# Audio tower layer: the feed-forward part in quads of sequences, or in rounds over a ring of pairs

## Chip, cores, metric

One core of a Trainium2 chip. The metric is the device time of one launch in microseconds (us). Four compute engines run side by side, each through its own queue in order: PE (matmul), DVE (vector), ACT (activation functions), POOL; SP issues the DMA transfers, also in order.

## What is computed

32 audio sequences of 313 frames of 512 samples go through a DCT, one retention-like attention block and one feed-forward block, each with a layernorm before it and a residual around it. The feed-forward block is what takes the time:

```python
h = tokenize(x)                                   # frames (32, 313, 512) times a 512x512 DCT
h = h + attn(layernorm(h))                        # 8 heads of 64, softmax times a decay matrix
y = layernorm(h)
theta = y[..., None, :] / (1 + abs(W)) + B_param  # (32, 313, 256, 512)
idx = mod(round(theta * 4096 / (2 * pi)), 4096)
cos_sum = sum(cos_table[idx] * attn_cos, axis=-1) # (32, 313, 256)
sin_sum = sum(sin_table[idx] * attn_sin, axis=-1)
h = h + silu(cos_sum @ proj_cos_w.T + sin_sum @ proj_sin_w.T)
```

So each of 256 hidden units needs a sine and a cosine of every feature of every frame: 32 x 313 x 512 x 256 x 2 = 2.6 billion function values.

## The kernel before

**Layout.** Features lie on the 128 partitions, in four chunks (NC4); frames lie along the free dimension. The 32 sequences are eight quads of four, so a chunk of a quad is a tile row of T = 4 x 313 = 1252 frames.

**Feed-forward, `ffn` (L538).** For each of 256 units n: four DVE operations (L556), one per chunk, turn `xT` (float32) into int16 indices with the unit's scale and bias per feature, `f_scale` and `f_bias`; L563 masks them to 12 bits for the sine; L568 and L574 add a quarter turn and mask again for the cosine, into a second buffer. ACT takes the sine of each whole buffer of 4 x 1252 = 5008 elements (L581). PE multiplies by `hot`, weights that are zero outside one column of 32 (L591), so that 32 units gather in one PSUM bank, each sequence in its own 32 rows. After 32 units DVE copies two banks out (L603) and SP stores them to `sums_d` in DRAM (L609). There are four index buffers, three of sine results, two of `hot`, four banks.

**Attention (`attention`, L293) and output (`output`, L493).** One sequence at a time: frames into `a5`, DCT (helper `rows`, L275), copy into `h` (L210), layernorm (L234, its inverse square root on POOL, L226 to L229), transpose, `xnT`, values `v`, gate, then two halves of four heads (`columns`, L289; scores L352; maxima L360; exponentials L378; transposes L399; decay L411; product with v L417), group norm (L440 to L456), the product with the gate, projection, residual (L475), a second layernorm, and the transposed result through `a5` to `xT_d` in DRAM. `load_xT` (L532) later reads a whole quad of it. The four copies out of PSUM into `h`, `xnT`, `v` and `a5` run on ACT (`ENG_H` and its like). `output` reads the sums back and finishes a sequence.

**Order.** Every step is entered into a `Plan` (L46) with a key, an engine, an estimated duration and the buffers that it reads and writes. `emit` (L63) runs through these once and fixes each engine's order: of the steps whose inputs would be ready, the one with the lowest key. The key of unit n of quad q is 512 q + 2 n, so a key step is one sine of 5008 elements. In `tile_audio_tower` the attention of quad 0 comes first, with two sets of buffers, A and B, two sequences at a time (L689). Then B's memory becomes that of the feed-forward part (`swap`, L692). While quad q is in the feed-forward part, attention of the four sequences of quad q+1 is spread over the keys between 30 and 482 of its 512 (L704); the last quad has no attention beside it.

Of the kernel before, what the change touches and what calls it, by code (L numbers as in the profile page):

```python
# [28 lines left out]
QUAD = 4  # L29
# [10 lines left out]
ENG_H = "ACT"  # L40
ENG_XNT = "ACT"
ENG_V = "ACT"
ENG_A5 = "ACT"
# [83 lines left out]
def tile_audio_tower(ctx: ExitStack, tc: tile.TileContext, t: dict, out: bass.AP):  # L127
    nc = tc.nc
    n_quads = t["frames"].shape[0]
    S = t["frames"].shape[4]  # L130
    T = QUAD * S
# [7 lines left out]
    out_v = out.rearrange("(a b) s d -> a b s d", b=QUAD)  # L139
# [9 lines left out]
    xT_d = dram.tile([P, NC4, T], F32, name="xT_d")  # L149
    sums_d = dram.tile([2, P, 2, T], F32, name="sums_d")  # L150
    wv_d = dram.tile([NC4, P, HOP], F32, name="wv_d")
    h_d = dram.tile([n_quads, QUAD, S, HOP], F32, name="h_d")

    class Buffers:


        def __init__(self, name, pool, psum):
# [8 lines left out]
            self.a5 = sb("a5", NC4, S)  # L166
            self.h = sb("h", NT, HOP)
            self.xn = sb("xn", NT, HOP)
            self.xnT = sb("xnT", NC4, S)
            self.v = sb("v", NT, HOP)  # L170
            self.gate = sb("gate", NC4, S)
            self.qk = [sb(f"qk{i}", 2, S) for i in range(2)]
            self.raw = sb("raw", 2, S)
            self.prob = sb("prob", NB, NT, S)
            self.probT = sb("probT", NT, S)
            wide = self.prob.rearrange("p a b s -> p (a b s)")
# [105 lines left out]
    def columns(plan, key, x, bank, src):  # L282

        k = x.load(plan, key, src)

        def go():
            w = x.ring[k].rearrange("p (c n) -> p c n", n=P)
            for c in range(NC4):
                nc.tensor.matmul(x.W[:, bank, :S], w[:, c, :], x.xnT[:, c, :],  # L289
                                 start=(c == 0), stop=(c == NC4 - 1))  # L290
        plan.add(key, "PE", 2200, go, (x.k("xnT"), x.k("ring", k)), x.banks(bank))

    def attention(plan, keys, q, b, x):  # L293
# [4 lines left out]
        def step(n=1.0):  # L298
            done[0] += n
            return keys(done[0] / 139.0)  # L300

        xns, probs = x.every("xn", NT), x.every("prob", NB)
        W3 = x.W[:N, :NT, :]
        plan.add(step(0), "SP", DMA_NS, lambda: nc.sync.dma_start(x.a5, t["frames"][q, b]), (),
                 (x.k("a5"),))
        rows(plan, step(7), x, x.a5, t["dct"], (x.k("a5"),))
        copy(plan, step(), ENG_H, NT * HOP, x.h[:N], W3, x.banks(0, 1, 2), (x.k("h"),))
        layernorm(plan, step(3), x)
        transposed(plan, step(3), x)
        copy(plan, step(), ENG_XNT, NC4 * S, x.xnT, x.W[:, :, :S], x.banks(0, 1, 2, 3), (x.k("xnT"),))  # L310
# [4 lines left out]
        copy(plan, step(), ENG_V, NT * HOP, x.v[:N], W3, x.banks(0, 1, 2), (x.k("v"),))  # L315
        plan.add(step(0), "POOL", 500, lambda: nc.gpsimd.memset(x.v[0:1, : NT - 1, :], 0.0), (),
                 (x.k("v"),))


        key = step(6)  # L320
        for g in range(NC4):
            columns(plan, key, x, g, t["wg"][g])
        plan.add(step(), "ACT", 1270,
                 lambda: nc.scalar.activation(x.gate, x.W[:, :, :S], AF.Silu),
                 x.banks(0, 1, 2, 3), (x.k("gate"),))

        for hb in range(H // NB):
            for g in range(hb * NB // 2, (hb + 1) * NB // 2):
                key = step(4)
                qk = x.qk[g % 2]  # L330
                kq = x.k("qk", g % 2)
# [12 lines left out]
                plan.add(key, "DVE", 1640, turned, x.banks(2, 3), (x.k("raw"), kq))  # L344
            for hd in range(hb * NB, (hb + 1) * NB):
                key = step(2.5)
                a, r0 = hd % NB, (hd % 2) * DH
                qk, kq = x.qk[hd // 2 % 2], x.k("qk", hd // 2 % 2)
# [39 lines left out]
            for hd in range(hb * NB, (hb + 1) * NB):  # L388
# [25 lines left out]
                for i in range(NT):  # L414
# [8 lines left out]
                    plan.add(key, "PE", 1000, go, (x.k("probT"), x.k("v")), x.banks(3))  # L423
# [9 lines left out]
                )  # L433

# [29 lines left out]
        for c in range(NC4):  # L464
# [6 lines left out]
                 lambda: nc.vector.tensor_tensor(x.gate, x.gate, x.aff, ALU.mult), probs,  # L471
                 (x.k("gate"),))
        rows(plan, step(7), x, x.gate, t["wo"], (x.k("gate"),))
# [18 lines left out]

    def output(plan, key, q, b, x):  # L493

        probs, xns = x.every("prob", NB), x.every("xn", NT)

        def load():
            for m in range(2):
# [328 lines left out]
```

## Time and profile before

| | |
|---|---|
| median of 3 runs | 19,201.89 us (19,189.18 to 19,209.79) |
| the profiled execution | 19,200.94 us, its span 19,199.2 us |
| ACT busy | 18,323.5 us (95%) |
| DVE busy | 17,754.5 us (92%) |
| PE busy | 14,967.9 us (78%) |
| DMA queue of SP | 806.95 MB, 14.3% of 16 engines' span |
| granted TensorE clock | 0.913 |

A row of the groups gives line, engine and operation, tiles written and read, shapes, count, then busy time in us and mean ns of one, then how long the engine sat idle just before such operations and what ended that. Successive operations of an engine overlap a little, so a mean is longer than the distance between two starts. The timeline gives start and length in us.

### The profile page before, as it was taken

What the parts mean: (1) busy time and instruction counts of PE and PEld (TensorE: products, weight loads), DVE (VectorE), ACT (ScalarE), POOL (GpSimd) and SP (SyncE); (2) the same over time, 40 slices, a digit from 0 to 9 for tenths busy, and PEclk for the clock granted to TensorE, in tenths of its full rate; (3) what the DMA queues carried; (4) which work ended last, traced back from release to release, by engine and by line L of the source; (5) the groups of instructions that cost most, each with busy time, mean ns of one, the idle gap of its engine ahead of it and who ended that gap; (6) DMA issues with size and microseconds to landing.
All of it is one profiled execution on the core that took longest, in us unless ns stands there. A gap on an engine that the chain in (4) does not pass through costs nothing.

```text
span 19199.2 us, 336270 instructions
## 1 busy us (share of the span) xinstructions
PE 14967.9 (78%) x148864; PEld 6732.7 (35%) x148864; DVE 17754.5 (92%) x17005; ACT 18323.5 (95%) x6051; POOL 581.0 (3%) x1222
## 2 busy tenths in 40 slices
PE   8777777887787877888777887788787777877666
PEld 5433333333333333333333333333333333322222
DVE  3799999999999999999999999999999999999997
ACT  1699999999999999999999999999999999999998
POOL 0000000000000000000000000000000000000000
PEclk8899999999999998999989999899999999987898
DMA  3111111111121111111111111111111111110001
GB/s 92 51 40 39 40 41 59 42 42 41 34 65 40 40 42 38 58 42 43 40 57 37 42 43 41 57 41 39 39 43 61 39 40 41 39 49 17 18 18 37
DMA packets 455954, 828.47 MB, mean 43 GB/s; under 512 B 54208, under 2 KB 103360, under 8 KB 454496
## 3 DMA queue, kind: packets, MB, share of 16 engines
q1 hardware_dynamic: 454496, 806.95, 14.3%
q8 instruction: 1169, 19.15, 0.4%
q14 instruction: 289, 2.37, 0.0%
HBM read 723.64 MB, written 83.10 MB: 42 GB/s over the span
## 4 chain that ended last, share of the span: by engine, by line
ACT 36%; DVE 33%; PE 17%; issue 11%; POOL 3%; DMA 0%; DVEq 0%; ACTq 0%; SPq 0%; POOLq 0%
ACT trig L581 34%; DVE ix L556 13%; PE pa L591 11%; DVE ix L563 5%; DVE ix L568 5%; DVE ix L574 5%; PE a_W L275 2%; PE a_W L289 2%; ACT a_prob L378 1%; DVE a_mx L360 1%; PE a_W L417 1%; PE a_W L352 1%; DVE a_prob L369 1%; POOL a_lu L226 1%; DVE a_st L238 0%
## 5 line engine op out<-in xcount | busy, mean ns | idle before, releaser
L581 ACT ACTIVATE trig<-ix 128x5008 f32<-128x5008 int16 x4096 | 17522.7, 4368 | 201.0 <-DVE ix L563 132.8
L591 PE MATMUL pa<-trig,hot 128*32 128x313 f32 x131072 | 10546.7, 468 | 3449.9 <-ACT trig L581 3433.5
L591 PEld LDWEIGHTS pa<-trig,hot 128*32 128x32 f32 x131072 | 4114.7, 117 | 9466.3 <-ACT trig L581 5200.6
L556 DVE TENSOR_SCALAR ix<-xT,f_scale,f_bias 128x1252 int16<-128x1252 f32 x8192 | 7108.7, 927 | 331.0 <-ACT trig L581 326.9
L568 DVE TENSOR_SCALAR ix<-ix 128x5008 int16<-128x5008 int16 x2048 | 3006.7, 1468 | 206.5 <-ACT trig L581 15.6
L563 DVE TENSOR_SCALAR ix<-ix 128x5008 int16<-128x5008 int16 x2048 | 2999.5, 1465 | 68.3
L574 DVE TENSOR_SCALAR ix<-ix 128x5008 int16<-128x5008 int16 x2048 | 3004.2, 1467 | 61.7
L289 PE MATMUL a_W<-a_xnT,a_ring 128*128 128x313 f32 x4800 | 1402.1, 437 | 92.2 <-DVE a_qk L338 66.6
L289 PEld LDWEIGHTS a_W<-a_xnT,a_ring 128*128 128x128 f32 x4800 | 873.3, 190 | 618.3 <-issue 156.1
L275 PE MATMUL a_W<-a_ring,a_a 128*105 128x512 f32 x1488 | 700.1, 612 | 27.5 <-DMA a_ring<-in_dct 15.4
L417 PEld LDWEIGHTS a_W<-a_v,a_probT 105*105 105x105 f32 x4320 | 482.7, 188 | 316.7 <-issue 187.5
L417 PE MATMUL a_W<-a_v,a_probT 105*105 105x64 f32 x4320 | 546.2, 277 | 41.1 <-DVE a_probT L411 41.0
L352 PE MATMUL a_W<-a_qk 64*105 64x313 f32 x1440 | 481.2, 459 | 100.8 <-DVE a_prob L369 75.9
L399 PE MATMUL a_W<-ident,a_prob 105*105 105x105 f32 x2160 | 350.4, 305 | 234.2 <-ACT a_prob L378 216.4
L275 PE MATMUL a_W<-a_ring,a_gate 128*105 128x512 f32 x720 | 377.0, 643 | 70.5 <-DVE a_gate L471 70.5
L399 PEld LDWEIGHTS a_W<-ident,a_prob 105*105 105x105 f32 x2160 | 282.0, 205 | 393.8 <-ACT a_prob L378 260.9
L275 PEld LDWEIGHTS a_W<-a_ring,a_a 128*105 128x105 f32 x1488 | 241.4, 173 | 419.4 <-issue 400.7
L275 PE MATMUL a_W<-a_ring,a_xnT 128*105 128x512 f32 x720 | 354.0, 616 | 2.8 <-ACT a_xnT L210 2.8
L226 POOL TENSOR_TENSOR a_gu<-a_gr 105x24 f32<-105x24 f32 x90 | 48.5, 539 | 10147.2 <-DVE a_gr L220 10142.5
L352 PEld LDWEIGHTS a_W<-a_qk 64*105 64x105 f32 x1440 | 224.1, 173 | 361.2 <-DVE a_prob L369 146.5
L262 PE MATMUL a_W<-ident,a_xn 105*128 105x105 f32 x1080 | 177.7, 291 | 172.5 <-DVE a_xn L250 90.1
L378 ACT ACTIVATE a_prob<-a_prob 105x313 f32<-105x313 f32 x540 | 242.6, 451 | 67.2 <-DVE a_prob L369 66.5
(136 smaller groups left out, 4029.3 us busy)
## 6 DMA issues: line engine op xcount, KB each, us to landing
hot<-in_hot SPq DMA_DIRECT2D x1024, 256.0 KB
a_dec<-in_decay SPq DMA_DIRECT2D x240, 260.5 KB
a_ring<-in_proj SPq DMA_DIRECT2D x128, 256.0 KB
a_ring<-in_dct SPq DMA_DIRECT2D x120, 256.0 KB
a_ring<-wv_d SPq DMA_DIRECT2D x120, 256.0 KB
a_ring<-in_wg SPq DMA_DIRECT2D x120, 256.0 KB
a_ring<-in_wq SPq DMA_DIRECT2D x120, 256.0 KB
a_ring<-in_wk SPq DMA_DIRECT2D x120, 256.0 KB
```

What stands on the lines that cost most here:

```text
L275: lambda c=c, i=i, k=k, to=to: nc.tensor.matmul(x.W[:N, to, :], lhsT[:, c, ROW0[i] : ROW0[i] + N], x.ring[k], start=(c == 0), stop=(c == N ...
L289: nc.tensor.matmul(x.W[:, bank, :S], w[:, c, :], x.xnT[:, c, :], start=(c == 0), stop=(c == NC4 - 1))
L352: lambda i=i, qk=qk, r0=r0: nc.tensor.matmul(x.W[:N, i, :S], qk[r0 : r0 + DH, 0, ROW0[i] : ROW0[i] + N], qk[r0 : r0 + DH, 1, :], start=Tru ...
L378: nc.scalar.activation(x.prob[:N, a, i, :], x.W[:N, i, :S] if last else x.prob[:N, a, i, :], AF.Exp, bias=m[:N, i : i + 1] if last else 0. ...
L399: nc.tensor.transpose(x.W[:N, jj, ROW0[i] : ROW0[i] + N], x.prob[:N, a, i, ROW0[j] : ROW0[j] + N], ident[:N, :N],)
L417: nc.tensor.matmul(x.y[:N, i, (hd % 2) * DH : (hd % 2 + 1) * DH], x.probT[:N, jj, ROW0[i] : ROW0[i] + N], x.v[:N, jj, hd * DH : (hd + 1) * ...
L556: nc.vector.tensor_scalar(now["ix", x][:, c, :], now["xT", c], f_scale[:, c, n : n + 1], f_bias[:, c, n : n + 1], ALU.mult, ALU.add)
L563: nc.vector.tensor_scalar(now["ix", x], now["ix", x], LUT - 1, LUT // 2, ALU.bitwise_and, ALU.bitwise_xor)
L568: nc.vector.tensor_scalar(new("ix", y, [P, NC4, T], I16, bufs=N_IX), now["ix", x], float(LUT // 4), None, ALU.add)
L574: nc.vector.tensor_scalar(now["ix", x], now["ix", x], LUT - 1, None, ALU.bitwise_and)
L581: nc.scalar.activation(new("trig", w, [P, NC4, T], bufs=N_TRIG), now["ix", x], AF.Sin, bias=-PI32, scale=ANG)
L591: nc.tensor.matmul(now["pa", p][b * 32 : b * 32 + 32, :S], now["hot", z][:, n % 2, c, k, :], now["trig", w][:, c, b * S : (b + 1) * S], st ...
```

## The change

**A ring of pairs.** A sequence pair is now the unit that enters. A ring has four places (`RING` = 8 sequences), each chunk of `xT` being one tile of 8 x 313 frames. The feed-forward part runs in rounds; a round takes 32 units (`UNITS`) for all pairs that stand in the ring, and a pair stays for eight rounds, that is 256 units, beginning with whichever block of 32 comes next. Pair p joins at round `STARTS[p]`: rounds 0 to 3 hold one pair, 4 to 9 two, 10 to 13 three, 14 to 35 four, 36 and 37 three, 38 and 39 two, 40 and 41 one. In rounds 36 to 39 an empty place lies between the pairs.

**Tile shapes in a round.** A buffer still has room for 16 x 313 = 5008 elements. With one pair it holds all eight combinations of four chunks and two units, with two pairs four of them, with four pairs two (one chunk, two units). With three pairs it also holds two, and so 3756 elements. An index operation covers all pairs of a chunk that are neighbours in the ring.

**Attention.** Only the first two sequences are done ahead, then `swap`. Buffers are shared: `u` takes the place of `a5`, `gate` and `qk`; `v` lies in `h`; `raw` in `probT`. Since `v` overwrites `h`, `h` is stored to DRAM after the DCT and read back after the heads; the gate is computed after the heads. The four copies out of PSUM run on DVE (`mover`), save for sequences whose attention begins while one pair is in the ring. `f_scale` and `f_bias` are computed in `prob`, stored to DRAM as `f_d` in eight blocks, and each round loads its block. Keys of attention are spread so that each pair is ready eight keys before its round; outputs stand before the next attention that begins.

```diff
-QUAD = 4
+RING = 8
+UNITS = 32
+SLOT = 16
+STARTS = (0, 4, 8, 10, 12, 14, 16, 18, 20, 22, 24, 26, 28, 30, 32, 34)
...
-            self.a5 = sb("a5", NC4, S)
+            self.u = sb("u", NC4, S)
+            self.qk = [self.u[:, 2 * i : 2 * i + 2, :] for i in range(2)]
             self.h = sb("h", NT, HOP)
+            self.v = self.h
...
+            self.raw = self.probT[:, 0:2, :]
...
-        copy(plan, step(), ENG_H, NT * HOP, x.h[:N], W3, x.banks(0, 1, 2), (x.k("h"),))
+        copy(plan, step(), mover, NT * HOP, x.h[:N], W3, x.banks(0, 1, 2), (x.k("h"),))
+        residual(step(0), False)
...
+        residual(step(0), True)
+        key = step(6)
+        for g in range(NC4):
+            columns(plan, key, x, g, t["wg"][g])
...
+    def ffn_round(plan, k0, blk, ring):
+        pairs = [(at, pair) for at, pair in enumerate(ring) if pair is not None]
+        r = 2 * len(pairs)
+        runs = []
+        for j, (at, _) in enumerate(pairs):
+            if runs and runs[-1][0] + runs[-1][2] == at:
+                runs[-1][2] += 1
+            else:
+                runs.append([at, j, 1])
+        n_p = min(SLOT // r, 2 * NC4) if SLOT % r == 0 else 2
+        E = n_p * r * S
...
+        for n in range(0, UNITS, 2):
...
+            todo = [(c, u) for c in range(NC4) for u in range(2)]
+            for i in range(n_slots):
+                parts = todo[i * n_p : (i + 1) * n_p]
...
+                                    nc.vector.tensor_scalar(
+                                        now["ix", x][:, d0 : d0 + 2 * m * S],
+                                        now["xT", c][:, 2 * at * S : 2 * (at + m) * S],
+                                        f[:, 0, c, n + u : n + u + 1], f[:, 1, c, n + u : n + u + 1],
+                                        ALU.mult, ALU.add)
...
+                        nc.scalar.activation(tl[:, :E], now["ix", x][:, :E], AF.Sin,
+                                             bias=-PI32, scale=ANG)
...
+                    key += n_p * r / SLOT
...
-    for b in range(QUAD):
-        attention(plan, lambda x: -1000.0 + b // 2 + x, 0, b, (A, B)[b % 2])
+    for b in range(2):
+        attention(plan, lambda x: -1000.0 + x, b, (A, B)[b], "ACT")
...
+    times, p, k = [], 1, 0.0
+    while p < len(STARTS):
+        due = [(key_of[STARTS[q]] - 8.0 - k) / (q - p + 1) for q in range(p, len(STARTS))]
+        for _ in range(int(np.argmin(due)) + 1):
+            times += [k, k + min(due) / 2]
+            k += min(due)
+            p += 1
...
+        narrow = sum(q is not None for q in rings[int(np.searchsorted(key_of, k, "right")) - 1]) <= 1
+        events.append((k, 1, lambda k=k, e=e, i=i, narrow=narrow: attention(
+            plan, lambda x: k + (e - k) * x, 2 + i, A, "ACT" if narrow else "DVE")))
```

With these keys the windows of attention are 60 keys for each of the sequences 2 and 3 (keys 0 to 120), 81 to 96 for 4 to 11 (to key 888), 113 or 128 for 12 to 31 (to key 3448). Round 4 begins at key 128, round 8 at 384, round 10 at 512, round 14 at 896, round 34 at 3456; the last round ends at 4096.

## The prediction

> **What bounds the kernel now.** I read the page's first two parts, then the groups by line, then the busy time in stretches, the timeline at the start and in the middle, and the waits inside the loop.
>
> ```profile
> PE 14967.9 (78%) x148864; PEld 6732.7 (35%) x148864; DVE 17754.5 (92%) x17005; ACT 18323.5 (95%) x6051; POOL 581.0 (3%) x1222
> ...
> L581 ACT ACTIVATE trig<-ix 128x5008 f32<-128x5008 int16 x4096 | 17522.7, 4368 | 201.0 <-DVE ix L563 132.8
> L556 DVE TENSOR_SCALAR ix<-xT,f_scale,f_bias 128x1252 int16<-128x1252 f32 x8192 | 7108.7, 927 | 331.0 <-ACT trig L581 326.9
> L568 DVE TENSOR_SCALAR ix<-ix 128x5008 int16<-128x5008 int16 x2048 | 3006.7, 1468 | 206.5 <-ACT trig L581 15.6
> ```
>
> ACT's 4096 sines (L581) are 17,523 of 19,199 us, and their element count is fixed by the problem. DVE, which makes their indices, is almost as full.
>
> ```profile
> 5000.00:10000.00 5000.00, 3939.75 (x39856) 1758.43 (x39851) 4755.58 (x4562) 4922.72 (x1620) 167.46 (x329) 0.92 0.15 44
> 18000.00:19000.00 1000.00, 624.49 (x7508) 238.20 (x7503) 922.66 (x830) 1000.00 (x235) 0.00 (x0) 0.90 0.06 18
> ```
>
> The columns are the stretch, its length, then busy time of PE, weight loads, DVE, ACT, POOL. In the middle ACT idles 1.5% and DVE 5%; in the last quad, which has no attention beside it, ACT idles not at all.
>
> ```profile
> 341.81 1.20 ACT L210 COPY b_a<-b_W 128x1252 f32<-128x1252 f32 x1 [9.58 <-PE b_W L262]
> 655.26 1.20 ACT L210 COPY b_a<-b_W 128x1252 f32<-128x1252 f32 x1 [9.59 <-PE b_W L262]
> 679.74 21.45 ACT L581 ACTIVATE trig<-ix 128x5008 f32<-128x5008 int16 x5 [10.57 <-DVE ix L563]
> ```
>
> The first pair's attention ends at 343 us, the second's at 656, and only 23 us later does the first sine start: 680 us with almost no sine work.
>
> ```profile
> 5005.23 3.45 DVE L556 TENSOR_SCALAR ix<-xT,f_scale,f_bias 128x1252 int16<-128x1252 f32 x4
> 5008.71 1.46 DVE L563 TENSOR_SCALAR ix<-ix 128x5008 int16<-128x5008 int16 x1
> 5010.28 1.47 DVE L568 TENSOR_SCALAR ix<-ix 128x5008 int16<-128x5008 int16 x1
> 5011.78 1.47 DVE L574 TENSOR_SCALAR ix<-ix 128x5008 int16<-128x5008 int16 x1
> ```
>
> From the chain that ended last, the start of two quads' first output:
>
> ```profile
> 3028.22 10.48 PE a_W L275 x24
> 5352.39 10.53 PE a_W L275 x24
> ```
>
> One unit costs DVE 5013.16 - 5005.23 = 7.93 us (its next instruction begins at 5013.16). Five sines take 21.43 us, the last at its full 4.37, so one takes 4.27 and a unit 8.54. Quads repeat every 2324 us (last two lines).
>
> ```profile
> L250 DVE TENSOR_SCALAR a_xn<-a_h,a_mv,a_lr 105x512 f32<-105x512 f32 x180 | 87.6, 542 | 131.8 <-POOL a_lr L229 131.8
> ```
>
> With the 1252-wide index (927 ns) this gives the slope of a DVE operation with two per-partition scalars: 385 ns / 740 elements = 0.52 ns, and 275 ns fixed. Back to back, (3.45 - 0.93) / 3 = 0.84 us each, so 0.19 us plus 0.52 ns per element.
>
> **Check on the old kernel.** ACT per sequence of attention: two blocks of exponentials at 8.35, three passes of 1.2 and three of 1.45, output 1.45: 26 us. A quad: 512 x 4.27 + 4 x 26 = 2289. DVE per sequence: the rows of the a_ buffers sum to 58 us, less 5 for overlap, plus 6 waiting for POOL's square roots (131.8 + 73.8 over 32): 59. A quad: 256 x 7.93 + 236 = 2267. Two nearly equal loads and a period of 2324: the coupling costs 1.5%.
>
> **What the Trainium skill says.** "VectorE: DVE Perf Modes", What auto-detection actually checks: a one-source operation in SBUF gets two elements a cycle if the outermost dimensions of source and destination are even or equal, four if both are also 16-bit. The 0.52 ns above agrees; all new widths (626, 1252, 1878, 2504; 3756) are even. "ScalarE: Activation LUTs", What ACT_TABLE_LOAD costs: 186 ns plus 0.833 per element with immediates, successors overlapping by 93. For 5008 that is 4358 against 4368 measured; a 3756-wide sine, which no row shows, I put at 3.22 us in a row. The int16 steps: 1467 ns at 5008 is 163 plus 0.26 per element, so 0.33 less at 3756.
>
> **The change, part by part.** I call "iteration" one index buffer and its two sines. A round is 32 units; 42 rounds hold 1 pair (rounds 0-3, 40-41), 2 (4-9, 38-39), 3 (10-13, 36-37) or 4 (14-35). The built program has 3520 sines of 5008 and 768 of 3756 elements instead of 4096: 192 more, 192 x 0.09 = 18 us.
>
> DVE per iteration, three int16 steps at 4.45 us together (3.47 at 3756): 1 pair, eight indices of 626: 8.70. 2 pairs, four of 1252: 7.93. 3 pairs, two of 1878: 5.93 against ACT's 6.45. 4 pairs, two of 2504: 2 x 0.19 + 2 x 1.30 with its end effects 3.11, so 7.56 against 8.54. Where a gap splits the ring: 6.31 (36-37) and 8.70 (38-39).
>
> Four copies of a sequence go from ACT to DVE for 27 of 30 sequences: ACT 26 - 5.2 = 20.8; DVE 59 + 6.2 = 65 (the 1536-wide PSUM pass L475 is 1.75 us, a 1252-wide 1.46).
>
> Now stage by stage, DVE's time first, ACT's second, the larger counts; the plan's keys give the sequences of attention in each. Start: the second pair's 313 us go; 343 + 23 + some 5 for the longer chain (gate after the heads, residual through DRAM) = 371. Rounds 0-3, 64 iterations and 2 sequences: 557 + 118 + 4 = 679 against 546 + 52 = 598, so 679. Rounds 4-7, 128 iterations, 2.67 sequences: 1015 + 171 + 4 = 1190 against 1150, so 1190. Rounds 8-9, 64 iterations, 1.33: 508 + 87 + 6 = 601 against 577, so 601. Rounds 10-13, 256 iterations, 4: 1518 + 260 + 12 = 1790 against 1651 + 86 = 1737, so 1790. Rounds 14-33, 1280 iterations, 20, with 18 outputs: 9677 + 1300 + 78 = 11,055 against 10,931 + 416 + 26 = 11,373; ACT sets it, with DVE 2.8% below. Without attention: rounds 34-35 ACT 1097, 36-37 ACT 832, 38-39 DVE 566, 40-41 DVE 284. End: the old last sine ends at 19,130, 69 us before the end, with four outputs 13 us apart; two fewer: 43.
>
> The sum is 18,826. For coupling I add 0.7% on rounds 0-33 (15,633 us), 109: the old kernel shows 1.5% at no slack and none in its last quad, where DVE has 7%; bounds 0 and 235. Outside the span lie 1.7 us. 18,937: I take 18,935. The profiled execution took 19,200.9 us, the median is 19,201.9, so nothing is to be scaled.
>
> **Edits costed at nothing.** PE: the matmuls of the sines stay 131,072, four at a time in different column groups. In rounds 0-3 it needs 64 x 2 x 2.31 + 2 x 138 = 572 of 679 us ((14,968 - 10,547) / 32 = 138 per sequence), so DVE covers it; without that cover it would cost what exceeds 679. Shared buffers (u, h with v, raw with probT) hold a sequence's steps back from each other: the next frames wait for the store of xT, the reload of h for the last product with v. In the narrowest window a sequence has 60 sines, 60 x 5.3 = 318 us, and a whole pair took 313 in the old start; a wide window has over 480. Bounds: 0, and 40 us if the first two sequences come late. DMA: one-hot loads fall from 1024 to 672; six stores and three loads of h per sequence replace three stores, and there are 42 small loads of coefficients. SP issues one in some 0.33 us and the DMA engines are 14% busy; the cover is that plan order puts each ahead of its use. The eight stores of coefficients stand in SP's queue behind ACT's and DVE's work on them, and the startup's ring loads behind those: bounds 0 and 10 us.
>
> **The added wait.** A joining pair's four xT loads wait in SP's queue for the store of xT; behind them stand one-hot loads and ring loads, behind those PE and then ACT. DVE's first index of the round waits for the load, with all later DVE work behind it. The old start prices it: store issued at 656.49, load issued at 666.05, first index at 672.59, so 16 us. The built order puts about two iterations, 15 us of DVE work, between the last copy and that index, and the filled index buffers feed ACT for up to 17 us more. So 0, with 8 us for each of 14 joins as the upper bound. The load also waits for the leaving pair's last index of its chunk, but with 4 pairs chunk 0 is read last eight sines before the round ends.
>
> **Rivals.** Coupling as before: the kernel planned both engines nearly full before too, and still lost 1.5%. Then 235 instead of 109, and half the joins' bound, 56: 18,826 + 291 = 19,117. For it: 2.8% of slack is little, and DVE gets bursts of attention. Against: the old loss belongs to zero slack.
>
> ACT alone counts: buffers absorb everything, coupling 0: 18,826.
>
> Late joins, slower than before: SP's queue is strictly in order and waited up to 29 us for PE before a one-hot load. If each join's loads or store are caught behind such waits, ACT runs dry at 14 joins. It decides from 54 us of path, against 16 seen: past 15 + 17 of cover, 22 us at each of 14 joins are 308, and 18,935 + 308 = 19,243.
>
> Odd halves, slower too: widths 626 and 1878 have odd halves (313, 939). If DVE then runs one element a cycle, 1878 costs 0.98 more: 256 x 2 x 0.98 = 501 in rounds 10-13, and 626 costs 0.33 more on 1536 instructions, 501, most of it on the path: about 19,850. The section of the Trainium skill named first speaks against it; the trace has no odd half.
>
> That the rounds don't pay as said: the start gains its 313 us in every case, since the first sine needs only two sequences; what can be lost is its return in rounds 0-13 (679 + 1190 + 601 + 1790 = 4260 for 28 pair-rounds, against 28 x 2324 / 16 = 4067 at the old rate: 193 us given back).
>
> **How the numbers follow.** Forecast 0.60, with its own range 18,870 to 19,010; coupling as before 0.22; ACT alone 0.10; late joins 0.05; odd halves 0.03. The range takes in the first three: below, ACT alone with 1% less DVE time in rounds 0-13 (43 us), 18,785; above, the coupling case to a little past its middle, 19,150. Left out are about a third of that case, the slower ones and the forecast's outer ends: 2 in 10. A change under 0.2% (38 us) can't be told from none with this kernel. Of the coupling case about a tenth, 0.02, lands within 0.2%: faster 0.90, same 0.02, slower 0.08.
>
> **What would show it.** First sine near 371 us. Index rows: 2504-wide near 1.58 us, 1878 near 1.25, 626 near 0.60; far more for the last two is the odd-half case. 3756-wide sines 3.3 us. Round 4 beginning near 1050, round 14 near 4630 us, with DVE over 97% busy between and ACT waiting for ix; from there to round 34 ACT over 98%, at about 1145 us per two rounds. Waits of DVE's index for xT beyond a few us at joins would be the late joins. I am wrong if ACT idles over 2% in rounds 14-33, or if the rounds before 14 take over 4500 us.

## The result, and the profile after

The changed kernel takes 19,079.31 us (19,069.93 to 19,093.18, four runs) against 19,195.53 us (19,188.64 to 19,209.79, four runs) for the kernel before: a ratio of 0.9939, 95% interval 0.9922 to 0.9956. That is 0.61% faster, where 1.4% was forecast. The profiled execution has a span of 19,077.0 us.

First the page's busy times. ACT is at 96%, so at first sight the change has filled it:

```profile
PE 14810.0 (78%) x148864; PEld 6622.6 (35%) x148864; DVE 17553.0 (92%) x15109; ACT 18228.6 (96%) x6133; POOL 660.5 (3%) x1222
```

The groups with the shapes kept apart show the new index widths and the shorter sine:

```profile
L595 DVE TENSOR_SCALAR ix<-xT,f 128x2504 int16<-128x2504 f32 x2816 | 4343.3, 1580 | 434.3 <-ACT trig L628 434.2
...
L628 ACT ACTIVATE trig<-ix 128x3756 f32<-128x3756 int16 x768 | 2485.6, 3320 | 99.4 <-PE pa L649 42.8 <-DVE ix L607 28.9 <-DVE ix L621 15.3
...
L595 DVE TENSOR_SCALAR ix<-xT,f 128x626 int16<-128x626 f32 x1536 | 833.3, 603 | 16.2 <-ACT trig L628 10.7 <-DMA xT<-xT_d 0.2
...
L595 DVE TENSOR_SCALAR ix<-xT,f 128x1878 int16<-128x1878 f32 x512 | 624.7, 1257 | 34.5 <-ACT trig L628 33.6
```

The timeline at the start has the first sine of the feed-forward part at 347.7 us; it was 679.7:

```profile
347.73 25.86 ACT L628 ACTIVATE trig<-ix 128x5008 f32<-128x5008 int16 x6 [8.84 <-DVE ix L607]
```

Now busy time by stage, the stretches cut at the first sine of rounds 0, 4, 10, 14 and 34 (stretch, length, then PE, weight loads, DVE, ACT, POOL):

```profile
347.70:1044.20 696.50, 565.98 (x5104) 284.00 (x5108) 655.85 (x860) 599.52 (x248) 37.94 (x76) 0.90 0.22 66
1044.20:2864.30 1820.10, 1475.00 (x14469) 692.48 (x14465) 1728.80 (x1683) 1728.71 (x613) 82.55 (x152) 0.93 0.17 51
2864.30:4701.10 1836.80, 1480.74 (x14493) 672.95 (x14486) 1715.43 (x1620) 1737.73 (x739) 81.27 (x152) 0.95 0.15 46
4701.10:16251.60 11550.50, 9188.56 (x92973) 4095.05 (x92971) 10723.38 (x8140) 11353.70 (x3700) 440.95 (x760) 0.93 0.13 39
16251.60:19032.30 2780.70, 1779.26 (x20672) 673.45 (x20672) 2587.71 (x2623) 2753.47 (x713) 0.00 (x0) 0.91 0.08 23
```

In rounds 14 to 33 (fourth row) ACT is busy 11,353.70 of 11,550.50 us and so idles 197 us, though DVE idles 827 us. Not all of that is slack, since DVE's busy time leaves out the short gaps between its operations and its waits for POOL. What shows slack is DVE's waits for ACT to free an index buffer, of which this is the larger part:

```profile
DVE ix L595 <- ACT trig L628: 327.4, 390, 3.1
```

With those at L615 they come to 372.5 us; DVE waits another 69.8 for PE and 5.5 for its own results. I call the rest of the stretch DVE's load: 11,103 us, 2.2% below ACT's 11,354. By the same count the old kernel has 2283 us against ACT's 2289 in a quad (first seven quads), 0.2% below.

The table sets each stretch against the kernel before, whose rate is 2324 us for a quad, that is 16 pair-rounds of 145.25 us.

| stretch | before, same work | forecast | after | after minus before |
|---|---|---|---|---|
| until the first sine | 679.7 | 371 | 347.7 | -332 |
| rounds 0-13, 28 pair-rounds | 4067 | 4260 + 30 | 4353.4 | +286 |
| rounds 14-33, 80 pair-rounds | 11,620 | 11,373 + 80 | 11,550.5 | -70 |
| rounds 34-41 and end | 2832.5 (the rest) | 2779 + 43 | 2825.4 | -7 |
| span | 19,199.2 | 18,936 | 19,077.0 | -122 |

The start gave more than was said, the narrow rounds took more of it back, and the steady part gained 70 us where 167 were expected. ACT's waits in rounds 14 to 33 (us in total, times, longest us), first of before in its loop from 3100 to 16,950 us, then of after:

```profile
ACT trig L581 <- DVE ix L563: 104.4, 69, 4.2
ACT trig L581 <- DVE ix L574: 41.4, 25, 2.2
ACT a_xn L510 <- PE a_W L275: 33.3, 13, 4.1
```

```profile
ACT trig L628 <- DVE ix L607: 72.2, 49, 4.2
ACT trig L628 <- DVE ix L621: 61.6, 30, 2.8
ACT trig L628 <- PE pa L649: 35.5, 19, 3.7
```

These two rows, with 3.5 us at L615, make 137 us. The third is a wait for PE (L649) to finish with a buffer of sine results. The sine still waits for its indices, first after the mask of a new buffer (L607) and then after the cosine's (L621). On average DVE is ahead; it falls behind somewhere. The timeline of DVE just after round 20 begins at 8162.5 us, where a new sequence's attention starts, and ACT's over the same time:

```profile
8171.73 1.75 DVE L210 COPY a_h<-a_W 105x1536 f32<-105x1536 f32 x1
...
8177.46 3.07 DVE L595 TENSOR_SCALAR ix<-xT,f 128x2504 int16<-128x2504 f32 x2
8180.57 1.47 DVE L607 TENSOR_SCALAR ix<-ix 128x5008 int16<-128x5008 int16 x1
8184.61 1.46 DVE L248 TENSOR_SCALAR a_xn<-a_h,a_mv,a_lr 105x512 f32<-105x512 f32 x3 [2.57 <-POOL a_lr L227]
```

```profile
8149.69 29.98 ACT L628 ACTIVATE trig<-ix 128x5008 f32<-128x5008 int16 x7
8182.15 4.38 ACT L628 ACTIVATE trig<-ix 128x5008 f32<-128x5008 int16 x1 [2.48 <-DVE ix L607]
8189.05 17.67 ACT L628 ACTIVATE trig<-ix 128x5008 f32<-128x5008 int16 x4 [2.52 <-DVE ix L621]
```

Read together: between the two index sets DVE copies the new frames out of PSUM, takes the layernorm's statistics, stands 2.57 us for POOL's square root (L227) and scales the frames (L248). From 8171.73 to 8188.85 that is 17 us, some 10 of them attention or waiting, with only one iteration of indices in it; ACT uses an iteration up every 8.6 us, runs dry, and loses 5.0 us. Going through all timelines of rounds 14 to 33, 104 of the 137 us that sines wait for DVE lie within 15 us of one of the 40 waits of L248 for POOL (two layernorms in each of 20 sequences), though these surroundings are about a tenth of the time.

My theory after this: the loss is set by the reserve, that is how many filled index buffers stand between DVE and ACT when such a cluster comes, and not by DVE's mean slack. The rival: it is set by the mean load of the two engines, so that work moved between them or taken away decides. The runs below are to tell these apart. The first expectations call the reserve theory "burst theory".

### The profile page after: what moved, and what is told of

Its sections match the earlier page's. It is cut to its first block, busy times and chain, and to the rows that moved or that the text cites. A ratio compares the mean times of both kernels' runs of the same rounds, so it can differ in the third digit from the quotient of the medians.

```text
span 19077.0 us, 333981 instructions
## 1 busy us (share of the span) xinstructions
PE 14810.0 (78%) x148864; PEld 6622.6 (35%) x148864; DVE 17553.0 (92%) x15109; ACT 18228.6 (96%) x6133; POOL 660.5 (3%) x1222
## 5 line engine op out<-in xcount | busy, mean ns | idle before, releaser
L628 ACT ACTIVATE trig<-ix 128x5008 f32<-128x5008 int16 (+1 forms) x4288 | 17551.6, 4178 | 476.8 <-DVE ix L607 169.0
L649 PE MATMUL pa<-trig,hot 128*32 128x313 f32 x131072 | 10341.3, 460 | 3135.8 <-ACT trig L628 3101.9
L649 PEld LDWEIGHTS pa<-trig,hot 128*32 128x32 f32 x131072 | 4052.9, 115 | 8977.3 <-ACT trig L628 4583.1
L595 DVE TENSOR_SCALAR ix<-xT,f 128x2504 int16<-128x2504 f32 (+3 forms) x5888 | 6673.6, 1184 | 499.8 <-ACT trig L628 493.3
L615 DVE TENSOR_SCALAR ix<-ix 128x5008 int16<-128x5008 int16 (+1 forms) x2144 | 3015.4, 1406 | 260.5 <-ACT trig L628 56.5
L607 DVE TENSOR_SCALAR ix<-ix 128x5008 int16<-128x5008 int16 (+1 forms) x2144 | 3028.8, 1413 | 69.3
L621 DVE TENSOR_SCALAR ix<-ix 128x5008 int16<-128x5008 int16 (+1 forms) x2144 | 3017.6, 1407 | 65.8
L273 PE MATMUL a_W<-a_ring,a_u 128*105 128x512 f32 x2256 | 1081.5, 615 | 102.4 <-DVE a_u L484 38.0
L355 PE MATMUL a_W<-a_u 64*105 64x313 f32 x1488 | 506.0, 464 | 141.6 <-DVE a_prob L372 134.9
L273 PEld LDWEIGHTS a_W<-a_ring,a_u 128*105 128x105 f32 x2256 | 358.3, 173 | 695.6 <-issue 593.7
L420 PEld LDWEIGHTS a_W<-a_h,a_probT 105*105 105x105 f32 x4464 | 487.6, 185 | 306.7 <-issue 206.0
L420 PE MATMUL a_W<-a_h,a_probT 105*105 105x64 f32 x4464 | 551.3, 274 | 39.5 <-DVE a_probT L414 39.3
L224 POOL TENSOR_TENSOR a_gu<-a_gr 105x24 f32<-105x24 f32 x93 | 59.5, 640 | 10761.4 <-DVE a_gr L218 10756.5
L355 PEld LDWEIGHTS a_W<-a_u 64*105 64x105 f32 x1488 | 232.8, 175 | 422.1 <-DVE a_prob L372 204.7
L414 DVE TENSOR_TENSOR a_probT<-a_W,a_dec 105x939 f32<-105x939 f32 x248 | 280.1, 1130 | 20.6 <-PE a_W L402 20.6
```

The costliest lines, as they stand in the source:

```text
L273: lambda c=c, i=i, k=k, to=to: nc.tensor.matmul(x.W[:N, to, :], lhsT[:, c, ROW0[i] : ROW0[i] + N], x.ring[k], start=(c == 0), stop=(c == N ...
L355: lambda i=i, qk=qk, r0=r0: nc.tensor.matmul(x.W[:N, i, :S], qk[r0 : r0 + DH, 0, ROW0[i] : ROW0[i] + N], qk[r0 : r0 + DH, 1, :], start=Tru ...
L414: nc.vector.tensor_tensor(x.probT[:N], x.W[:N, :NT, :S], w3, ALU.mult)
L420: nc.tensor.matmul(x.y[:N, i, (hd % 2) * DH : (hd % 2 + 1) * DH], x.probT[:N, jj, ROW0[i] : ROW0[i] + N], x.v[:N, jj, hd * DH : (hd + 1) * ...
L595: nc.vector.tensor_scalar(now["ix", x][:, d0 : d0 + 2 * m * S], now["xT", c][:, 2 * at * S : 2 * (at + m) * S], f[:, 0, c, n + u : n + u + ...
L607: nc.vector.tensor_scalar(tl, tl, LUT - 1, LUT // 2, ALU.bitwise_and, ALU.bitwise_xor)
```

## Experiments

The edits are against the changed kernel. "Idle" is ACT's idle time in rounds 14 to 33 unless another stretch is named; it is 197 us there after the change.

**Cluster: tell the planner that POOL's square root is slow.** The built order then puts more index work between L218 and L248.

```diff
-        plan.add(key, "POOL", 3500, newton, (kv,), (kr, ku))
+        plan.add(key, "POOL", 7000, newton, (kv,), (kr, ku))
```

> The changed kernel with one number altered in the plan: the Newton steps on POOL are planned at 7.0 us (what they take) instead of 3.5, so the order puts more index work between an inverse square root's start and the DVE step that waits for it. Burst theory (ACT idles in rounds 14-33 because clusters of attention steps, the wait for POOL among them, outlast the index buffers): DVE's 244 us of waits for POOL fall below 60, ACT's 196 us of idling in rounds 14-33 fall to about 100, the whole to about 18,960. Load theory (DVE's mean load of 97% is what costs): the waits move elsewhere, at most 30 us gained, 19,050.

Measured: 19,077.1 us, 0.9937 (0.9922 to 0.9951), idle 178. No gain. ACT's waits in rounds 14 to 33:

```profile
ACT trig L628 <- PE pa L649: 57.8, 35, 5.0
ACT a_xn L516 <- PE a_W L273: 53.9, 9, 7.1
ACT trig L628 <- DVE ix L607: 30.5, 39, 2.3
```

The time is what the load theory expected and 117 us above what the burst theory did. The waits for indices did fall, from 137 to 39 us, so the order around the cluster decides them. But 68 us came back as waits for PE: the output's silu (L516) from 7.8 to 53.9 us, the sine buffers (L649) from 35.5 to 57.8. And POOL got slower. Its middle step, in the groups of after and then of this run:

```profile
L225 POOL TENSOR_TENSOR a_lu<-a_lu,a_lv 105x3 f32<-105x3 f32 x186 | 103.5, 556 | 14.6
```

```profile
L225 POOL TENSOR_TENSOR a_lu<-a_lu,a_lv 105x3 f32<-105x3 f32 x186 | 166.2, 894 | 14.6
```

The same 105x3 operation rose from 556 to 894 ns on average: the more index work stands beside it, the longer it takes, so DVE's waits for POOL's L227 and L466 fell only from 161 to 115 us in these rounds; over the whole they fell from 245 to 162 where under 60 was expected.

**Load: the four copies on ACT for all sequences.**

```diff
-            plan, lambda x: k + (e - k) * x, 2 + i, A, "ACT" if narrow else "DVE")))
+            plan, lambda x: k + (e - k) * x, 2 + i, A, "ACT")))
```

> The changed kernel with the four copies out of PSUM of every sequence on ACT again, as in the kernel before. ACT gets 27 x 5.2 = 140 us more, DVE 27 x 6.2 = 167 us less. Load theory: DVE then has 5% slack in rounds 14-33, ACT's idling there nearly ends (196 to under 60), so the whole is about 19,080 + 104 - 140 = 19,050, and 30 to 60 us better in the DVE-bound rounds 4-13. Burst theory: the copies are 6 us in clusters of over 15, idling falls by a third at most, the whole ends at about 19,080 + 104 - 65 = 19,120.

Measured: 19,072.7 us, 0.9935 (0.9918 to 0.9952); rounds 4-9 1801.2, 10-13 1829.0 us. Rounds 14 to 33:

```profile
4675.20:16249.70 11574.50, 9201.35 (x92974) 4115.31 (x92972) 10611.09 (x8060) 11442.99 (x3779) 423.93 (x760) 0.93 0.14 39
```

ACT has 89 us more to do and idles 65 us less (131.5): the stretch is only 24 us longer. In the narrow rounds, where DVE sets the pace, ACT's copies save 27 us together. So this part of the change is worth nothing over the whole: of the 89 us that it takes from ACT 65 come back as idling, and the rest is lost in the narrow rounds. Idling fell by a third, as the burst theory had it, but the time lies between the two theories' times and doesn't decide.

**Reserve: three index buffers instead of four.**

```diff
-    N_IX, N_TRIG, N_HOT, N_PA = 4, 3, 2, 4
+    N_IX, N_TRIG, N_HOT, N_PA = 3, 3, 2, 4
```

> The changed kernel with three index buffers instead of four (five do not fit). Burst theory: ACT's reserve shrinks from two iterations to one and a half, its idling in rounds 14-33 grows from 196 us to over 400, the whole to over 19,300. Load theory: mean loads are the same, idling 196 to at most 260, the whole under 19,160.

Measured: 19,280.7 us, 1.0043 (1.0028 to 1.0058).

```profile
4771.10:16437.50 11666.40, 9232.27 (x92971) 4117.56 (x92969) 10722.40 (x8140) 11361.35 (x3700) 448.01 (x760) 0.92 0.13 39
```

DVE's and ACT's work is what it was (10,722 and 11,361 us), yet idle is 305 us instead of 197. One buffer costs 201 us in all, more than the whole gain of the change. The size is short of what the reserve theory expected, but the load theory has no reason for it. Here and in every run below with another number of buffers one thing more changes: the buffers enter `emit`, which then fixes another order. Of some 8140 DVE operations in rounds 14 to 33 about 570 stand elsewhere with three buffers, about 600 with six. So the runs show what buffers are worth with the order built for them, not room by itself; but the first run, whose order differs from the changed kernel's as much, gained nothing.

**Order: DVE's feed-forward steps ahead by eight keys in the rounds of four pairs.**

```diff
+        lead = 8.0 if r == RING else 0.0
...
-                                plan.add(key, "DVE", 233 + 0.521 * 2 * m * S, index,
+                                plan.add(key - lead, "DVE", 233 + 0.521 * 2 * m * S, index,
```

and so for the three int16 steps.

> The changed kernel; in rounds with four pairs the DVE steps of the feed-forward part get a key 8 lower, so that the order fills the index buffers first and fits attention into what is left. Burst theory: clusters meet full buffers, ACT's idling in rounds 14-33 falls from 196 to under 80 us, the whole to about 18,960. Load theory: no change beyond 30 us, or attention comes late at joins and the whole is over 19,100.

Measured: 19,463.2 us, 1.0138 (1.0123 to 1.0154), idle about 570 of 11,928 us: much slower, which only the load theory's late joins had allowed for. A joining pair is now late. DVE's waits, and DVE and then ACT at one join:

```profile
DVE ix L596 <- DMA xT<-xT_d: 35.9, 11, 5.2
```

```profile
8253.35 3.08 DVE L596 TENSOR_SCALAR ix<-xT,f 128x2504 int16<-128x2504 f32 x2 [4.02 <-DMA xT<-xT_d]
```

```profile
8258.04 17.18 ACT L629 ACTIVATE trig<-ix 128x5008 f32<-128x5008 int16 x4 [8.11 <-DVE ix L608]
...
8290.33 12.92 ACT L629 ACTIVATE trig<-ix 128x5008 f32<-128x5008 int16 x3 [9.72 <-PE pa L650]
```

The store of `xT` is issued at 8244.6, the load at 8249.2, the first index runs at 8253.4: 9 us of path with nothing left to cover it. ACT idles 16 to 20 us at a join (10 at the first), 5 to 7 in the changed kernel. So the rival of late joins names a real mechanism; with the order as built it doesn't act (DVE waited 0.2 us for `xT` in the whole changed kernel). But the ten joins hold only 174 of the 570 us. In 241 us, the largest group of ACT's waits, the trace shows nothing that ACT waited for, and why they come is open. Here a lead in the keys made no reserve.

**Room for more buffers: half of the ring.** Four index buffers fill the memory. To free 20 KB of a partition I left out part of the computation, as the expectation says; a joining pair then loads two chunks instead of four.

```diff
-        for c in range(NC4):
-            new("xT", c, [P, RING * S], bufs=NC4)
+        for c in range(2):
+            new("xT", c, [P, RING * S], bufs=2)
...
-                                        now["xT", c][:, 2 * at * S : 2 * (at + m) * S],
+                                        now["xT", c % 2][:, 2 * at * S : 2 * (at + m) * S],
```

> The changed kernel with two of the four feature chunks left out of the ring: chunks 2 and 3 take their indices from the tiles of chunks 0 and 1, every instruction of DVE, ACT and PE stays. It frees 20 KB per partition and serves as the base of the two next runs. Both theories: like the changed kernel, 19,080 plus or minus 20, ACT idling about 196 us in rounds 14-33.

Measured: 19,075.0 us, 0.9935 (0.992 to 0.995), idle 203. DVE's operations stand in the same order in rounds 14 to 33, and the time is the same, so it can serve as a base.

**Six index buffers on that base** (`N_IX = 6`).

> As the base with half the ring, with six index buffers instead of four. If clusters on DVE outlast the index buffers (three buffers: 304 us of idling in rounds 14-33, four: 196), idling falls below 100 and the whole by over 100 us. If the trigger is PE holding the sine buffers, idling stays over 160 and the whole gains under 40.

Measured: 18,995.3 us, 0.9895 (0.988 to 0.9909).

```profile
4695.00:16172.70 11477.70, 9228.37 (x92978) 4097.99 (x92977) 10721.25 (x8143) 11344.81 (x3699) 452.49 (x760) 0.93 0.14 39
```

```profile
ACT a_xn L516 <- PE a_W L273: 54.1, 9, 7.2
ACT trig L628 <- issue: 30.5, 22, 2.0
ACT trig L628 <- PE pa L649: 20.9, 19, 3.7
ACT trig L628 <- DVE ix L621: 5.0, 4, 2.6
```

The waits for DVE fall from 133 in the base to 9 us, with DVE's busy time the same to 4 us: no mean was touched, and this cause is gone. The sizes fell short: the whole gains 80 us where over 100 were expected, and idle is still 133 us where under 100 was. Nine output silus now wait 54 us for PE; as I read it, ACT, no longer late, reaches them before PE is ready.

**Four sine buffers on that base** (`N_TRIG = 4`), a reserve between ACT and PE instead.

> As the base with half the ring, with four buffers of sine results instead of three. If PE, held up in its queue by attention steps, is what stops ACT, idling in rounds 0-33 (484 us) falls by over 150. If DVE's index reserve is, it gains only the waits that the trace puts down to PE: 35 us in rounds 14-33 and at most 125 before.

Measured: 19,025.5 us, 0.991 (0.9893 to 0.9926), idle 172. Rounds 0-3, 4-9, 10-13 take 686.1, 1810.1, 1835.5 us. The waits for indices stay (73.4 + 66.2 us), and idling in rounds 0-33 falls from 487 in the base to 438, not by over 150. A smaller gain (50 us) by another way; it doesn't touch the main loss.

**Width: index operations over at most two pairs.**

```diff
-            if runs and runs[-1][0] + runs[-1][2] == at:
+            if runs and runs[-1][0] + runs[-1][2] == at and runs[-1][2] < 2:
```

> The changed kernel with index operations of at most two pairs (1252 elements), so the wide index alone undone. DVE gets 0.37 us per iteration more in rounds 10-35 (about 1664 iterations, 620 us in all). By my sum DVE then needs 1106 + 47 = 1153 us for two rounds of 14-33 against ACT's 1137 and sets the pace: with 1% of coupling 1165, so ten times 10 us more and 110 in rounds 10-13, the whole about 19,290. If DVE's load didn't matter at all in rounds 14-33 it would be 19,190.

Measured: 19,309.8 us, 1.0058 (1.0043 to 1.0073); two rounds take 1172.6 us, idle 361. DVE's load in rounds 14 to 33, counted as above, is 11,557 us (1156 for two rounds, where the sum said 1153) and so above ACT's 11,366. The time follows it, somewhat further above it than the 1% that I allowed. DVE's waits for a free index buffer fall to a third:

```profile
DVE ix L595 <- ACT trig L628: 119.3, 189, 1.3
```

The wide index is worth 230 us: this part of the change pays.

**The old schedule in the new program, copies on ACT.** Four sequences ahead and quads, but shared buffers, `h` through DRAM and coefficients by blocks. The list of attention times begins with the third pair accordingly.

```diff
-STARTS = (0, 4, 8, 10, 12, 14, 16, 18, 20, 22, 24, 26, 28, 30, 32, 34)
+STARTS = (0, 0, 8, 8, 16, 16, 24, 24, 32, 32, 40, 40, 48, 48, 56, 56)
...
-    for b in range(2):
-        attention(plan, lambda x: -1000.0 + x, b, (A, B)[b], "ACT")
+    for b in range(4):
+        attention(plan, lambda x: -1000.0 + b // 2 + x, b, (A, B)[b % 2], "ACT")
...
-            plan, lambda x: k + (e - k) * x, 2 + i, A, "ACT" if narrow else "DVE")))
+            plan, lambda x: k + (e - k) * x, 4 + i, A, "ACT")))
```

> The changed program made to run the old schedule: pairs join two at a time every eight rounds, four sequences of attention ahead, the four copies on ACT. What is left of the change is the sharing of attention buffers and the coefficients by round. Both theories: these cost and bring nothing, 19,200 plus or minus 30.

Measured: 19,235.9 us, 1.0018 (1.0012 to 1.0025). Quads take 2331 to 2335 us instead of 2323 to 2326, and ACT idles 272 us in seven quads instead of 230. The first sine comes 24 us sooner (655.7 us instead of 679.7), and the seven quads take 54 us longer. So the buffers and what they carry cost 34 us in all, and the ring itself is worth 163 us: the ring with the copies on ACT too took 19,072.7.

**The same with the copies on DVE** (`"DVE"` in the last line).

> As the run before, with the four copies on DVE: the moved copies alone, in quads. ACT gets 146 us less, DVE 174 us more, so DVE needs 2267 + 25 = 2292 per quad against ACT's 2268. Reserve theory (attention reaches DVE in clusters, and what a cluster exceeds the index buffers' reserve by goes to ACT): longer clusters, ACT's idling per quad grows from 36 by more than the 21 it is relieved of, 19,220 to 19,300. Load theory: the larger mean load is 2292 instead of 2289, the same time, 19,200 to 19,220.

Measured: 19,341.6 us, 1.0073 (1.0056 to 1.009). ACT's waits in the loop, of the run with the copies on ACT and then of this one:

```profile
ACT trig L628 <- DVE ix L607: 121.1, 125, 2.9
ACT trig L628 <- DVE ix L621: 108.6, 85, 2.3
```

```profile
ACT trig L628 <- DVE ix L607: 306.4, 243, 4.3
ACT trig L628 <- DVE ix L621: 155.3, 106, 3.0
```

The four copies add 106 us to the old schedule, more than both theories had it. Part of that is load: DVE's is 2310 us a quad, not the 2292 of the sum, and well above ACT's 2273; quads take 2345. So the run doesn't tell the theories apart. I take it that the ring's wide index made room for the copies.

**Copies on DVE only beside four pairs** (`<= 1` becomes `<= 3` in the line of `narrow`).

> The changed kernel with the four copies on ACT in all rounds with three pairs or fewer, on DVE with four. Rounds 4-13 as in the run with all copies on ACT (27 us better there), rounds 14-33 as in the changed kernel: 19,050.

Measured: 19,058.8 us, 0.9926 (0.9911 to 0.994); rounds 4-9 1801.7, 10-13 1827.6, idle 191. The 28 us that the copies cost in the narrow rounds are saved; the total is 21 us lower.

**A complete version with a fifth index buffer.** It is the previous edit, and the two rotation tables lie in the decay buffers and are loaded again for each half of the heads, which frees the room.

```diff
-    N_IX, N_TRIG, N_HOT, N_PA = 4, 3, 2, 4
+    N_IX, N_TRIG, N_HOT, N_PA = 5, 3, 2, 4
...
-            self.dec = [sb(f"dec{i}", STEP * (NT - 1) + S) for i in range(2)]
+            self.dec = [sb(f"dec{i}", 2 * S) for i in range(2)]
...
+            for d, name in enumerate(("cos_qk", "sin_qk")):
+                plan.add(step(0), "SP", DMA_NS,
+                         lambda d=d, name=name: nc.sync.dma_start(
+                             x.dec[d].rearrange("p (a s) -> p a s", s=S), t[name]),
+                         (), (x.k("dec", d),))
...
-    cos_qk = load("cos_qk", 2, S)
-    sin_qk = load("sin_qk", 2, S)
```

> As the run before, with five index buffers; the room comes from keeping the two rotation tables in the buffers of the decay matrices, loaded anew twice per sequence (8 us of transfers on SP's queue each time, off ACT's path). Reserve theory: between 203 us of idling in rounds 14-33 with four buffers and 133 with six, so 165, and some 10 us before: 19,050 - 45 = about 19,005. Load theory: 19,050. If the four extra loads hold up attention, over 19,060.

Measured: 18,980.9 us (18,973.4 to 18,986.6), 0.9884 (0.987 to 0.9899): the best version, 98 us below the changed kernel. Rounds 14 to 33, then ACT's waits in them:

```profile
4680.00:16148.50 11468.50, 9297.22 (x92977) 4141.77 (x92979) 10707.38 (x8136) 11350.60 (x3703) 437.09 (x760) 0.92 0.14 42
```

```profile
ACT trig L635 <- PE pa L656: 43.4, 40, 3.7
ACT a_xn L523 <- PE a_W L273: 42.6, 13, 5.6
```

Idle is 118 us, waits for DVE 8 us. One buffer more takes nearly all of the loss to waits for indices. Of the 98 us the buffer brings 78 and the placing of the copies, already in the run before, 21; 45 were expected of the buffer.

**Old schedule with six index buffers,** the rival's last ground: that the reserve helps only where DVE has slack. It joins the edits of the old schedule, the half ring and `N_IX = 6`.

> The run in quads with the copies on ACT (19,236 us, ACT idle 272 us in seven quads), with half the ring left out as before (chunks 2 and 3 take indices from the tiles of 0 and 1) and six index buffers. If only the reserve counts, its DVE waits (230 us) go to under 40 although DVE has hardly any slack: about 19,050. If slack is needed for a reserve to fill, they stay over 120, and the whole over 19,130.

Measured: 19,163.3 us, 0.9984 (0.9977 to 0.9991). Waits for indices fall from 230 to 43 us, nearly as the reserve theory expected, but idle only from 272 to 210.5, and the whole stays above the 19,130 of the other branch:

```profile
ACT a_xn L516 <- PE a_W L273: 56.2, 11, 9.3
ACT a_xnT L208 <- PE a_W L260: 32.3, 14, 3.7
ACT trig L628 <- DVE ix L607: 25.5, 37, 1.2
ACT trig L628 <- DVE ix L621: 17.2, 12, 2.2
```

The gain of 73 us is about that in the ring (80 us, 19,075.0 to 18,995.3). I expected more: ACT's own waits for PE, which hold 89 us of these lines, were not in my account.

**Narrow index with six buffers** (the width's edit, half ring, `N_IX = 6`), to see where mean load takes over.

> The run with the narrow index operations (19,310 us), with half the ring left out and six index buffers. By my sum DVE needs 1153 us for two rounds of 14-33 and ACT 1137. If the sum is right, the reserve can't bring them below 1153: 20 rounds at 11,530 to 11,600 instead of 11,727, the whole 19,120 to 19,190. If mean load is no limit here, 11,480 as with wide operations and six buffers, the whole about 19,030.

Measured: 19,156.3 us, 0.9979 (0.9971 to 0.9986); two rounds take 1158 us where DVE's sum says 1153, idle 224. Six buffers save 153 us here, but the time stops 161 us above the same buffers with the wide index. DVE hardly ever finds the index buffers full any more:

```profile
DVE ix L595 <- ACT trig L628: 22.9, 32, 1.3
```

Its load is 11,515 of 11,581 us. Here mean load is a floor; the reserve decides how far above it the kernel stays.

**What follows.** In rounds 14 to 33, with both engines' work the same within 17 us, ACT idles 305, 197 (203 with half the ring), 118 and 133 us for three, four, five and six index buffers. The sixth shows no gain over the fifth, though these two stand on different bases: what is left is mostly waits for PE in ACT's order of work. The reserve theory holds for the waits on DVE, with the order built for the buffers; alone it doesn't account for all idling, and the load theory keeps the floor. A fifth index buffer together with a fourth sine buffer was not tried.

## Why the prediction was right and wrong

**Right: the loads.** ACT's load in rounds 14 to 33 was put at 11,373 us and is 11,354. The new durations, 1.58, 1.25, 0.60 and 3.3 us, are 1580, 1257, 603 and 3320 ns. Odd halves don't slow DVE: the Trainium skill's page "VectorE: DVE Perf Modes", What auto-detection actually checks, which asks for outermost dimensions that are even or equal, agrees with the trace at 626 and 1878. Rounds 34 to 41 took 2781 us against 2779, the end 45 against 43. DVE's load, counted as above, was put at 4260 us in rounds 0 to 13 and 11,055 in rounds 14 to 33, and is 4255 and 11,103.

**Right: no late joins.** The path is covered as worked out, and the run with the lead shows what late joins cost: 174 us of idling at ten joins against 54.

**Near: the start.** 348 instead of 371. The 5 us added for a longer chain weren't needed, and the old schedule in the new program also started 24 us sooner, so the rest seems to come with the new program and not with the ring.

**Wrong: "For coupling I add 0.7% on rounds 0-33 (15,633 us), 109".** The bounds for these rounds sum to 15,633 us and the rounds took 15,903.9: 271 us more, 1.7%. In rounds 14 to 33 it is 178 us over the bound against 80, in rounds 0 to 13 93 against 30. The forecast missed the profiled span by 142; the coupling term fell short by 162, and 20 came back at the start and end. The step that failed is this term: it prices the coupling by mean slack, between the old kernel's 1.5% at none and nothing at 7%, and with it goes the sentence against the rival, "the old loss belongs to zero slack". Slack did rise about as worked out, from 0.2% to 2.2% (the forecast had 1% and 2.8%; its 2267 us for DVE in an old quad are 16 too few), yet ACT's idling rose from 1.4% to 1.7% of its work. What the runs showed in place of slack is the reserve: with both loads the same within 17 us, idling was 305, 197, 118 and 133 us for three, four, five and six index buffers. Four buffers are two iterations, 17 us of sines, whatever the mean slack; in the trace 104 of 137 us of waiting lie at the two layernorms of each sequence. The last quad, from which I took "none" at 7% slack, has no attention, so no clusters: it was not a point on a curve of slack. The rival "coupling as before" had the right size: 18,826 + 235 is 19,061 before its joins, which cost nothing for waits on loads. The measured time lies inside the range that I gave because that rival was taken into it; the forecast's own range of 18,870 to 19,010 missed.

**Wrong, small: "Shared buffers" at 0.** The old schedule in the new program costs 34 us more. The upper bound of 40 was meant for two late sequences at the start; that it covers a loss that in the run lies in the quads is luck. Which of the edits that it joins costs them wasn't separated.

**Wrong, and hidden in the sum: the copies moved to DVE.** I priced them as a gain for ACT of 5.2 us a sequence and a cost for DVE of 6.2. In rounds 14 to 33 ACT was relieved of 89 us, of which the time kept 24; in the narrow rounds they cost 27. Net nothing.

**The sign for being wrong.** I had named ACT idle over 2% in rounds 14 to 33 (it was 1.7%) or over 4500 us before round 14 (4701 minus 348 is 4353; from the span's start 4701). The first bar was set above the loss that was to be told apart, the second didn't say from where it counts. DVE was to be over 97% busy in rounds 4 to 13: by busy time it was 94%, by its load 98%.

**Left open.** Rounds 0 to 13 took 93 us over their bound. Copies on ACT save 28 of these, a fourth sine buffer 18 against its base, six index buffers 6. DVE sets the pace there and still waits 61 us for ACT and 36 for PE; the rest wasn't separated. Why the output's silu comes to wait just when ACT is no longer late was read from the waits and not tried.

## What to carry to other kernels

Where two engines in series are each over 90% full, don't price their coupling by mean slack alone: find the longest stretch in which the feeding engine does other work, compare it with what the filled buffers hold, and count how often it comes. One more buffer can be worth more than moving work (78 us with the fifth index buffer and 21 with the copies placed to suit, none from four copies moved in all rounds). When the wait named first is taken away, look which in-order wait stands behind it before counting the gain.

## What the runs showed of the hardware

POOL's small operations stretch beside DVE. The timeline of POOL at the cluster shown above:

```profile
8177.63 1.46 POOL L224 TENSOR_TENSOR a_lu<-a_lr 105x3 f32<-105x3 f32 x1 [45.76 <-DVE a_lr L218]
8179.17 1.42 POOL L225 TENSOR_TENSOR a_lu<-a_lu,a_lv 105x3 f32<-105x3 f32 x1
8180.67 1.42 POOL L226 TENSOR_SCALAR a_lu<-a_lu 105x3 f32<-105x3 f32 x1
8182.17 0.19 POOL L227 TENSOR_TENSOR a_lr<-a_lr,a_lu 105x3 f32<-105x3 f32 x1
```

An operation on 105x3 elements takes 0.19 us while DVE stands still (from 8182.0 to 8184.6) and 1.4 us beside an index or mask operation, about the length of one of these. The whole trace agrees: of 744 such operations in `a_lr`'s chain (L224 to L227), the 531 that begin while no DVE operation runs take 0.19 us on average, and so do 13 that begin beside a copy of the sums out of PSUM (L666); the 200 that begin beside an index or mask operation take 1.2 to 1.4 us on average, according to its line. The Trainium skill, "SBUF — State Buffer", SBUF: two separate sides, says that DVE in a two-port mode and GpSimd share a port pair under an exclusive lock held for the whole instruction; the trace agrees as far as it shows this: the operation begun at 8180.67 ends at 8182.09, the mask beside it (L607, shown above) at 8182.04. So index work put into DVE's wait for POOL lengthens POOL's chain and takes back part of the gain: POOL's busy time rose from 660.5 to 935.4 us in the first experiment.
